# The first product of a macaron block's start: its weights on two transfer queues, and TensorE's order around it

## Chip, cores and metric

One core of a Trainium2 chip runs the whole program in one launch. The metric is the device time of one execution in microseconds, as the median over a number of executions; smaller is better. Beside the timed runs there is one execution with the hardware profiler on.

## What is computed

Tokens x of shape (2, 2048, 256), all in float32, go through three residual steps: half a grouped feed-forward step, a state-space step, and the same feed-forward step again.

```python
x = x + 0.5 * ffn(layernorm(x), W1, b1, W2, b2)
x = x + ssm(layernorm(x), Wi, bi, conv_w, conv_b, Wdt, bdt, A_log, Bm, Cm, Dv, Wo, bo)
x = x + 0.5 * ffn(layernorm(x), W1, b1, W2, b2)
```

The feed-forward step cuts the 4096 tokens into 8 groups of 512. Group g has its own weights, and there is no nonlinearity between its two products:

```python
h1 = einsum('gmh,goh->gmo', xg, W1) + b1[:, None, :]     # 256 -> 1024
h2 = einsum('gmo,gho->gmh', h1, W2) + b2[:, None, :]     # 1024 -> 256
```

The state-space step projects 256 channels to 2 x 512, runs a causal convolution of width 4 and a SiLU over the first half, makes a step size with a softplus, and scans 512 channels with 16 states each over the 2048 tokens of a sequence. The scan's output is gated with SiLU of the other half and projected back to 256 channels; the normalised input times the mean of Dv is added.

## The kernel before

The tokens are worked on in four blocks (s) of 1024, two blocks to a sequence. A block has two halves (h) of 512 tokens, and a half of the tokens is also one group of the feed-forward step: g = 2s + h.

Since the feed-forward step has no nonlinearity, the kernel first multiplies the two weight arrays of a group into one 256 x 256 array. combine(g, k, hh) does this on TensorE: k is one of the two halves of the 1024 inner channels, hh one of the two halves of the 256 input channels, and each call is four matmuls, which in float32 are two passes each. k = 0 and k = 1 add up in the same PSUM tile, pwc. combined(g) brings it to SBUF as wc, scaled by 0.5: ScalarE takes hh = 0, and in group 0 VectorE takes hh = 1. The bias row b1 W2 + b2 is made on TensorE as well. pad_bias copies a group's b1 into a padded tile (GpSimd), bias_pe multiplies it with the second weight array (four matmuls for each k, then one for b2, which lands in the same tile pbc), and bias_act copies the row to SBUF (ScalarE). For group 0 the row is added inside the token product: product(pair, True) multiplies 256 transposed tokens with wc and then spreads the row over the partitions (line 402 and line 298).

A half of the tokens is made ready by settle (statistics on VectorE, two small steps on ScalarE for the root, then the normalisation, one pair of token tiles on VectorE and the other on ScalarE) and by turn (four TensorE transposes for each pair, line 370, and a ScalarE copy to SBUF).

What the core reads at the start is issued in the order of the code. load_x(s, h) issues one transfer of 512 KB of tokens, in pieces of 1 KB. load_w(g, k) issues two transfers of 512 KB, one for each weight array (lines 121 and 122), in pieces of 4 KB. SP's queue gets the first tokens, then the weights of group 0, k = 0 and k = 1, then those of group 1, then wi_sb, the input projection (line 149). ScalarE's queue gets b1 (line 144) and the second half's tokens. GpSimd's queue gets b2 early and, after pad_bias(0), the parameters of the state-space step (load_par).

TensorE's order at the start is the order in which the code is written, by hand. busy(n) issues n matmuls of zeros (line 769). Then come the transposes of the first half, the product for k = 0, the first part of the bias row, the product for k = 1, the second part of the bias row, and then the token product. The transposes of the second half and the weights of group 1 follow, and the first projection of the state-space step.

```python
    busy(12)
    settle(first[0])
    turn(first[0])
    for hh in range(2):
        combine(0, 0, hh)
    settle(first[1])
    pad_bias(0)
    load_par()
    make_sel_rep()
    bias_pe(0, (0,))
    for hh in range(2):
        combine(0, 1, hh)
    combined(0, True)
    bias_pe(0, (1,))
    bias_act(0)
```

Behind the start a loop runs over 256 steps t, one scan of 1024 elements on 128 partitions each (line 691). For each step a plan says which other pieces of work are issued with it; the dictionary PL gives the distance of each piece from a base step, and a name such as nw or tp0 stands there once for all blocks. at(t, fn) puts a piece into the plan, and put_ffn, put_second and put_prepare put whole chains of them. The weights of later groups are issued from the plan, too, by load_w, through SP's queue.

Of the kernel before, what the change touches and what calls it, by code (L numbers as in the profile page):

```python
# [74 lines left out]
def macaron_kernel(ctx: ExitStack, tc: tile.TileContext, x, wi_t, wo_t, wdt_t, par, w1, w2_t, b1, b2, bo, out):  # L75
    nc = tc.nc
    V, S, T, GP = nc.vector, nc.scalar, nc.tensor, nc.gpsimd
# [62 lines left out]
    wo_sb = const.tile([P, NPAIR, DM], F32, name="wo_sb")  # L140

    load_x(0, 0)
    load_w(0, 0)
    S.dma_start(b1_sb, b1.rearrange("p g o -> p (g o)"))
    load_x(0, 1, S)
    load_w(0, 1)
    for k in range(2):
# [619 lines left out]
    def busy(n, warm=warm):  # L767
        for _ in range(n):
            T.matmul(warm[:, :DM], lhsT=zeros[:, :P], rhs=zeros, start=True, stop=True)
# [17 lines left out]
    bias_pe(0, (0,))
    for hh in range(2):
        combine(0, 1, hh)
    combined(0, True)  # L790
    bias_pe(0, (1,))
    bias_act(0)
    make_par_g()
    make_neg_a()
    for pair in range(2):
# [50 lines left out]
    plan = {}

    def at(t, fn, *a, name=None):

        name = name or fn.__name__  # L850
        kind = 3 if name == "fill" else 2 if name in ("dt_pe", "dt_act", "exp_table") else name.endswith("_pe") or name in (
            "product", "project_out", "combine")
        if t % 1:
            kind = 4
        plan.setdefault(int(t), []).append((kind, lambda: fn(*a)))

    def put(t, make, *steps):
# [4 lines left out]
            at(t + d, lambda method=method, a=a: getattr(box[0], method)(*a), name=method)  # L862

    def put_ffn(t, s, h, name):
        put(t, lambda: Ffn(s, h, name), (0, "stats"), (PL["nw"], "newton", GP), (PL["nr"], "normalise", 0, GP),
            (PL["nr"], "normalise", 1, GP), (PL["tp0"], "turn_pe", 0), (PL["ta0"], "turn_act", 0),
            (PL["tp1"], "turn_pe", 1), (PL["ta1"], "turn_act", 1), (PL["bi"], "bias", GP), (PL["pr0"], "product", 0),
            (PL["pr1"], "product", 1), (PL["ad0"], "add_act", 0), (PL["ad0"], "add_gp", 0),
            (PL["ad1"], "add_act", 1), (PL["ad1"], "add_gp", 1))
# [5 lines left out]

    def put_prepare(t, s, q):
        if (s, q) == (0, 1):
            put(t, lambda: Prepare(s, q), (5.5, "inner_pe", 0), (5.5, "inner_pe", 1), (6, "start_xi"), (6, "inner_act", 0),
                (6, "inner_act", 1), (6, "edges"), (6, "centre", 0), (7, "centre", 1),
                (PL["z0"], "tap", 2, 0), (PL["z1"], "tap", 1, 0), (PL["z2"], "tap", 0, 0), (PL["z2"], "gate_u", 0),  # L880
                (PL["z3"], "drive_gp", 0),
                (PL["y0"], "tap", 2, 1), (PL["y1"], "tap", 1, 1), (PL["y2"], "tap", 0, 1), (PL["y2"], "gate_u", 1),
                (PL["y3"], "drive_gp", 1), (PL["y4"], "gate_pe", 0), (PL["y4"], "gate_pe", 1), (PL["y5"], "silu_zs"))
            return
        steps = [(PL["i0"], "inner_pe", 0), (PL["i1"], "inner_pe", 1), (PL["ia"], "start_xi"), (PL["ia"], "inner_act", 0),
                 (PL["ia"], "inner_act", 1), (PL["ed"], "edges"), (PL["ce"], "centre", 0), (PL["ce"], "centre", 1)]
        steps += [(PL["tp"] + n, "tap", k, i)
                  for n, (k, i) in enumerate((k, i) for k in (2, 1, 0) for i in range(NJ2))]
        steps += [(PL["g0"], "gate_pe", 0), (PL["g1"], "gate_pe", 1), (PL["si"], "silu"),
                  (PL["dr"], "drive", GP, 0), (PL["dr"], "drive", GP, 1)]  # L890
# [30 lines left out]
    for s in range(NB):  # L921
# [24 lines left out]
        if s + 1 < NB:
            for h in range(2):
                t = e + PL["f3" + "ab"[h]]
                put_ffn(t, s, h, "f3")
                at(t + PL["st"], store, s, h)  # L950
            g = 2 * s + 2
            for h in range(2):
                at(b + PL[f"lx{h}"] if s > 0 else b + 2 + h, load_x, s + 1, h)
# [4 lines left out]
                at(c + PL["bp"], bias_pe, g + h)
                at(c + PL["cb"], combined, g + h)
                at(c + PL["ba"], bias_act, g + h)  # L960
                at(c + PL["sp"], spread_pe, g + h)
                at(c + PL["sq"], spread_act, g + h)
# [126 lines left out]
```

## Time and profile before

| what | value |
|---|---|
| median of 3 runs | 771.52 us (767.36 to 773.42) |
| profiled execution, its own time | 764.32 us |
| span from its first to its last instruction | 762.5 us |
| mean granted TensorE clock | 0.937 |
| TensorE busy | 642.3 us (84%) |
| VectorE busy | 638.6 us (84%) |
| ScalarE busy | 527.1 us (69%) |
| GpSimd busy | 512.9 us (67%) |
| traffic of the DMA engines | 62.29 MB, mean 82 GB/s |
| first tokens: issue, landing | 0.73 us, 4.7 us |
| weights of group 0 (w1 and w2 of k = 0, then of k = 1): landings | 6.6, 9.8, 11.4 and 12.9 us |
| second half's tokens: issue, landing | 1.22 us, 12.5 us |
| first scan starts | 42.22 us |

Times inside an execution count from the first instruction of the span. A landing is the time of issue and the time from issue to landing that the profile gives. A busy time of TensorE counts passes that overlap in its pipeline, so it isn't work at its peak.

### The profile page before, as it was taken

Reading aid. Unit: us, or ns where it says so; the run is one execution under the profiler, and the core shown is the slowest. Engines: PE = TensorE matmul, PEld = TensorE weight load, DVE = VectorE, ACT = ScalarE, POOL = GpSimd, SP = SyncE. Lnnn points to the kernel's source line nnn. Section 1 sums busy time; section 2 is a strip of 40 time slices with the busy share of each in tenths; the row PEclk is TensorE's granted clock in tenths of the full one; section 3 lists DMA queues with packets and bytes.
Section 4 is the critical chain, followed back from the end, with each engine's and each line's share of the span. In section 5 each row is a group of like instructions: output and inputs, shape, how many; then the busy total and the mean of one; then the engine's idle time right before and its main releaser. Section 6 shows DMA issues by size and latency. Waiting matters only on the chain.

```text
span 762.5 us, 10406 instructions
## 1 busy us (share of the span) xinstructions
PE 642.3 (84%) x3428; PEld 277.1 (36%) x3428; DVE 638.6 (84%) x553; ACT 527.1 (69%) x658; POOL 512.9 (67%) x821
## 2 busy tenths in 40 slices
PE   9999795993879998897888998897697989677966
PEld 7634241440212543542211643353121524212534
DVE  3587777793999989776999989776999999999995
ACT  3467885753899576765899675757699777768631
POOL 5125658899854759979853779989964678753321
PEclk9999799997899999999899999999799999897989
DMA  8274216242122325415122325313122222322101
GB/s 298 72 220 113 55 29 166 56 125 68 28 56 65 74 56 155 135 38 160 40 55 56 73 67 142 112 51 75 37 56 55 56 57 75 92 56 55 29 1 55
DMA packets 42789, 62.29 MB, mean 82 GB/s; under 512 B 12536, under 2 KB 22128, under 8 KB 42736
## 3 DMA queue, kind: packets, MB, share of 16 engines
q1 hardware_dynamic: 41344, 59.84, 28.9%
q0 software_dynamic: 720, 1.24, 0.6%
q8 instruction: 27, 0.44, 0.2%
q10 hardware_dynamic: 672, 0.56, 0.2%
q14 instruction: 26, 0.21, 0.1%
HBM read 24.08 MB, written 4.19 MB: 37 GB/s over the span
## 4 chain that ended last, share of the span: by engine, by line
PE 39%; POOL 22%; DVE 13%; ACT 11%; issue 6%; DMA 6%; SPq 2%; ACTq 0%; DVEq 0%; POOLq 0%
DVE g L691 11%; PE pwc L259 7%; PE py L700 7%; PE po L732 7%; POOL u L530 5%; ACT dec L678 5%; PE pv L662 4%; DMA rep<-dt 3%; PE pf_f L402 3%; PE pxi L488 3%; POOL tap L529 3%; DMA w<-in_w_t 2%; POOL x L414 2%; POOL x L395 2%; PE pz L488 2%
## 5 line engine op out<-in xcount | busy, mean ns | idle before, releaser
L678 ACT ACTIVATE dec<-rep,neg_a 128x1024 f32<-128x1024 f32 (+1 forms) x280 | 287.6, 1059 | 122.4 <-DVE g L691 82.9
L691 DVE TENSOR_TENSOR_SCAN g<-dec,state,pv 128x1024 f32<-128x1024 f32 (+1 forms) x160 | 309.5, 2003 | 26.6 <-PE py L700 13.0
L691 DVE TENSOR_TENSOR_SCAN g<-dec,pv 128x1024 f32<-128x1024 f32 (+1 forms) x128 | 264.9, 2131 | 34.4 <-PE py L700 17.2
L700 PE MATMUL py<-g,wy 128*32 128x512 f32 x1024 | 167.7, 654 | 51.1 <-ACT ev_y L707 35.0
L530 POOL TENSOR_TENSOR u<-u,tap 128x512 f32<-128x512 f32 x90 | 114.2, 1268 | 9.0 <-ACT u L524 1.6
L662 PE MATMUL pv<-v,sel_rep 64*128 64x512 f32 (+1 forms) x256 | 72.8, 663 | 31.9 <-POOL v L630 15.2
L693 POOL COPY state<-g 128x1 f32<-128x1 f32 x160 | 27.5, 185 | 80.0 <-DVE g L691 80.0
L700 PEld LDWEIGHTS py<-g,wy 128*32 128x32 f32 x1024 | 25.2, 111 | 147.4 <-issue 60.6
L711 POOL TENSOR_TENSOR z<-ev_y,z 128x512 f32<-128x512 f32 x31 | 39.6, 1276 | 50.3 <-ACT ev_y L707 50.3
L402 PE MATMUL pf_f<-wc,xnt_f 128*128 128x256 f32 x256 | 66.5, 405 | 5.9 <-ACT ev_f L410 4.3
L529 POOL TENSOR_SCALAR tap<-xi,par_p 128x512 f32<-128x512 f32 x84 | 58.1, 692 | 8.7 <-DMA xi<-xi 5.4
L488 PE MATMUL pz<-xn2t,wi_sb 128*64 128x512 f32 x224 | 61.9, 681 | 0.0
L259 PE MATMUL pwc<-w,w 128*128 128x256 f32 x256 | 60.8, 386 | 0.2 <-ACT dt L94 0.2
L402 PEld LDWEIGHTS pf_f<-wc,xnt_f 128*128 128x128 f32 x256 | 48.0, 197 | 32.5 <-ACT ev_f L410 8.2
L732 PE MATMUL po<-wo_sb,z 64*128 64x256 f32 x448 | 54.6, 391 | 0.8 <-POOL z L711 0.7
L259 PEld LDWEIGHTS pwc<-w,w 128*128 128x128 f32 x256 | 47.1, 190 | 18.4 <-issue 8.9
L488 PE MATMUL pxi<-xn2t,wi_sb 128*64 128x512 f32 x224 | 51.1, 598 | 0.0
L732 PEld LDWEIGHTS po<-wo_sb,z 64*128 64x128 f32 x448 | 43.5, 192 | 16.8 <-issue 10.6
L395 POOL TENSOR_TENSOR x<-x,bc 128x1024 f32<-128x1024 f32 x14 | 33.0, 2355 | 23.4 <-ACT xn_f L361 23.4
L662 PEld LDWEIGHTS pv<-v,sel_rep 64*128 64x128 f32 (+1 forms) x256 | 19.6, 190 | 75.6 <-DVE g L691 35.3
L630 POOL TENSOR_TENSOR v<-u,dt 128x512 f32<-128x512 f32 x28 | 35.0, 1270 | 6.9 <-ACT u L597 6.9
L414 POOL TENSOR_TENSOR x<-ev_f,x 128x512 f32<-128x512 f32 x24 | 30.4, 1269 | 3.1 <-ACT ev_f L410 3.1
(158 smaller groups left out, 745.1 us busy)
## 6 DMA issues: line engine op xcount, KB each, us to landing
rep<-dt SPq DMA_DIRECT2D x496, 64.0 KB, 2.0
w<-in_w SPq DMA_DIRECT2D x16, 512.0 KB, 6.9
w<-in_w_t SPq DMA_DIRECT2D x16, 512.0 KB, 8.7
x<-in_x SPq DMA_DIRECT2D x7, 512.0 KB, 3.9
out<-x SPq DMA_DIRECT2D x6, 512.0 KB, 3.2
wi_sb<-in_wi_t SPq DMA_DIRECT2D x1, 1024.0 KB, 13.8
wo_sb<-in_wo_t SPq DMA_DIRECT2D x2, 512.0 KB, 6.7
out<-x SPq DMA_DIRECT2D x4, 256.0 KB, 2.2
```

What stands on the lines that cost most here:

```text
L259: T.matmul(pt, lhsT=a[:, oc, hh * P : (hh + 1) * P], rhs=b[:, oc, :], start=(k == 0 and oc == 0), stop=(k == 1 and oc == NO // 2 - 1),)
L395: eng.tensor_tensor(self.xs, self.xs, bc[self.g].to_broadcast((P, GT, DM)), ALU.add)
L402: T.matmul(o, lhsT=self.xt[pair][:, hh, k * P : (k + 1) * P], rhs=wc[self.g][:, hh, :], start=(hh == 0), stop=(hh == NH - 1 and not bias))
L414: GP.tensor_tensor(part, self.ev.rearrange("p (a b) -> p a b", a=2), part, ALU.add)
L488: T.matmul(pt[h * HC : (h + 1) * HC, :], lhsT=wi_sb[:, hh, k : k + HC], rhs=xn2t[self.s, h][:, hh, :], start=(hh == 0), stop=(hh == NH - 1))
L529: GP.tensor_scalar(tap, self.xi[:, u, k : k + CH], self.par(C_CW, NK, u, k), 0.0, ALU.mult, ALU.add)
L530: GP.tensor_tensor(self.u[:, u, :], self.u[:, u, :], tap, ALU.add)
L662: T.matmul(t[:, c * CH : (c + 1) * CH], lhsT=sel_rep[r, c if is_wide(s, j) else a, :], rhs=v_sb[s, j // NJ2][r, j % NJ2, :], start=True, s ...
L678: S.activation(decs[t][:, c * w : (c + 1) * w], part, AF.Exp, scale=neg_a[:, i : i + 1])
L691: V.tensor_tensor_scan(g[:, r], dec[:, r], v[:, r], 0.0 if first else state[:, i : i + 1], ALU.mult, ALU.add)
L700: T.matmul(pys[s, j][rows(is_wide(s, j), a, c), :], lhsT=wy[:, column(s, j, a, c, m), :], rhs=gs[a, m][:, c * CH : (c + 1) * CH], start=(m ...
L732: T.matmul(held_po[s, pair][h][:, k * DM : (k + 1) * DM], lhsT=lhsT, rhs=rhs, start=((q, i) == parts[0]), stop=((q, i) == parts[-1]))
```

## The change

Three things are changed.

The transfers at the start: load_w takes a queue for the second weight array. For group 0 this is ScalarE's queue: w1 of k = 0 and k = 1 go on SP's queue behind the first tokens, w2 of k = 0 and k = 1 go on ScalarE's queue, ahead of b1 and of the second half's tokens.

TensorE's order at the start: eleven matmuls of zeros in place of twelve, then the product for k = 0, the transposes of the first half, the whole bias row, and the product for k = 1. ScalarE copies the bias row ahead of wc.

The plan: each chain gets names of its own in PL (f3a.nw, f1b.nw, q2.t3 and so on), each with the value that the shared name had, and the weights of later groups are issued by load_w_part, one array at a time.

```diff
-    def load_w(g, k, pool=None):
+    def load_w(g, k, pool=None, second=nc.sync):
...
         nc.sync.dma_start(a, w1v[:, k * NO // 2 : (k + 1) * NO // 2, :])
-        nc.sync.dma_start(b, w2v[:, k * NO // 2 : (k + 1) * NO // 2, :])
+        second.dma_start(b, w2v[:, k * NO // 2 : (k + 1) * NO // 2, :])
         w_sb[g, k] = (a, b)
...
     load_x(0, 0)
-    load_w(0, 0)
+    for k in range(2):
+        load_w(0, k, second=S)
     S.dma_start(b1_sb, b1.rearrange("p g o -> p (g o)"))
     load_x(0, 1, S)
-    load_w(0, 1)
     for k in range(2):
         load_w(1, k, p5)
     nc.sync.dma_start(wi_sb, wi_t.rearrange("(hh p) d -> p hh d", p=P))
+
+    def load_w_part(g, k, i):
+
+        view = (w1, w2_t)[i][g].rearrange("(p oc) h -> p oc h", p=P)
+        a = wpool.tile([P, NO // 2, DM], F32, tag=f"w{i + 1}", name=f"w{i + 1}_{g}_{k}")
+        nc.sync.dma_start(a, view[:, k * NO // 2 : (k + 1) * NO // 2, :])
+        w_sb[g, k] = (*w_sb.get((g, k), ()), a)
...
-    busy(12)
+    busy(11)
     settle(first[0])
-    turn(first[0])
+    pad_bias(0)
     for hh in range(2):
         combine(0, 0, hh)
+    turn(first[0])
     settle(first[1])
-    pad_bias(0)
     load_par()
     make_sel_rep()
-    bias_pe(0, (0,))
+    bias_pe(0)
+    bias_act(0)
     for hh in range(2):
         combine(0, 1, hh)
     combined(0, True)
-    bias_pe(0, (1,))
-    bias_act(0)
...
-                    for k in range(2):
-                        at(c + PL["lw"], load_w, g + h + 1, k)
+                    for n in range(4):
+                        at(c + PL[f"w{n}"], load_w_part, g + h + 1, n // 2, n % 2)
```

More of the change, by code (lines that the diff above doesn't have):

```diff
@@ L842, in macaron_kernel @@
         load_w(2, k)
-    PL = {'g0': 8, 'g1': 11, 'si': 12, 'po0': 3, 'po1': 7, 'poa': 4, 'c0': 12, 'c1': 28, 'f3a': 13, 'f3b': 17, 'f1a': 20, 'f1b': 30, 'sa': 32, 'sb': 41, 'nw': 0, 'nr': 2, 'tp0': 3, 'ta0': 5, 'tp1': 4, 'ta1': 6, 'bi': 7, 'pr0': 7, 'pr1': 8, 'ad0': 9, 'ad1': 10, 'rs': 3, 'rb': 7, 'i0': 0, 'i1': 0, 'ia': 2, 'ed': 2, 'ce': 3, 'tp': 5, 'dr': 12, 'dv0': 4, 'dv1': 7, 'cb': 8, 'bp': 2, 'ba': 5, 'sp': 8, 'sq': 9, 'lw': 6, 'lx0': 16, 'lx1': 28, 'st': 12, 'r0': 0, 'r1': 4, 'xg0': 2, 'xs0': 5, 'xf0': 7, 'xf1': 16, 'xg1': 8, 'xs1': 14, 'xw': 23, 'xp0': 12, 'xp1': 29, 'xd': 18, 'xr0': 29, 'xb0': 35, 'xr1': 32, 'xb1': 40, 'y0': 11, 'y1': 12, 'y2': 13, 'y3': 17, 'y4': 16, 'y5': 18, 'z0': 6, 'z1': 8, 'z2': 8, 'z3': 10, 'ga': 2, 'gm': 2, 'eo': 3, 'en': 4, 'ep': 6, 'eb': 8, 'u0': 1, 'u1': 1, 'u2': 1, 'u3': 2, 'u4': 3, 'u5': 4, 'u6': 5, 'u7': 5, 'u8': 6, 'u9': 7, 'ua': 11}
+    PL = {'po0': 3, 'po1': 7, 'c0': 12, 'c1': 28, 'f3a': 13, 'f3b': 17, 'f1a': 20, 'f1b': 30, 'sa': 32, 'sb': 41, 'dv0': 4, 'dv1': 7, 'lx0': 16, 'lx1': 28, 'st': 12, 'r0': 0, 'r1': 4, 'xg0': 2, 'xs0': 5, 'xf0': 7, 'xf1': 16, 'xg1': 8, 'xs1': 14, 'xw': 23, 'xp0': 12, 'xp1': 29, 'xd': 18, 'xr0': 29, 'xb0': 35, 'xr1': 32, 'xb1': 40, 'y0': 11, 'y1': 12, 'y2': 13, 'y3': 17, 'y4': 16, 'y5': 18, 'z0': 6, 'z1': 8, 'z2': 8, 'z3': 10, 'ga': 2, 'gm': 2, 'eo': 3, 'en': 4, 'ep': 6, 'eb': 8, 'u0': 1, 'u1': 1, 'u2': 1, 'u3': 2, 'u4': 3, 'u5': 4, 'u6': 5, 'u7': 5, 'u8': 6, 'u9': 7, 'ua': 11, 'f3a.nw': 0, 'f3a.nr': 2, 'f3a.tp0': 3, 'f3a.ta0': 5, 'f3a.tp1': 4, 'f3a.ta1': 6, 'f3a.bi': 7, 'f3a.pr0': 7, 'f3a.pr1': 8, 'f3a.ev0': 9, 'f3a.ad0': 9, 'f3a.ev1': 10, 'f3a.ad1': 10, 'f3a.nr1': 2, 'f3b.nw': 0, 'f3b.nr': 2, 'f3b.tp0': 3, 'f3b.ta0': 5, 'f3b.tp1': 4, 'f3b.ta1': 6, 'f3b.bi': 7, 'f3b.pr0': 7, 'f3b.pr1': 8, 'f3b.ev0': 9, 'f3b.ad0': 9, 'f3b.ev1': 10, 'f3b.ad1': 10, 'f3b.nr1': 2, 'f1a.nw': 0, 'f1a.nr': 2, 'f1a.tp0': 3, 'f1a.ta0': 5, 'f1a.tp1': 4, 'f1a.ta1': 6, 'f1a.bi': 7, 'f1a.pr0': 7, 'f1a.pr1': 8, 'f1a.ev0': 9, 'f1a.ad0': 9, 'f1a.ev1': 10, 'f1a.ad1': 10, 'f1a.nr1': 2, 'f1b.nw': 0, 'f1b.nr': 2, 'f1b.tp0': 3, 'f1b.ta0': 5, 'f1b.tp1': 4, 'f1b.ta1': 6, 'f1b.bi': 7, 'f1b.pr0': 7, 'f1b.pr1': 8, 'f1b.ev0': 9, 'f1b.ad0': 9, 'f1b.ev1': 10, 'f1b.ad1': 10, 'f1b.nr1': 2, 'sa.nw': 0, 'sa.nr': 2, 'sa.tp0': 3, 'sa.ta0': 5, 'sa.tp1': 4, 'sa.ta1': 6, 'sa.rs': 3, 'sa.rb': 7, 'sa.nr1': 2, 'sb.nw': 0, 'sb.nr': 2, 'sb.tp0': 3, 'sb.ta0': 5, 'sb.tp1': 4, 'sb.ta1': 6, 'sb.rs': 3, 'sb.rb': 7, 'sb.nr1': 2, 'q1.i1': 0, 'q1.ia': 2, 'q1.ed': 2, 'q1.ce': 3, 'q1.g0': 8, 'q1.g1': 11, 'q1.si': 12, 'q1.dr': 12, 'q1.t0': 5, 'q1.t1': 6, 'q1.t2': 7, 'q1.t3': 8, 'q1.t4': 9, 'q1.t5': 10, 'q2.i0': 0, 'q2.i1': 0, 'q2.ia': 2, 'q2.ed': 2, 'q2.ce': 3, 'q2.g0': 8, 'q2.g1': 11, 'q2.si': 12, 'q2.dr': 12, 'q2.t0': 5, 'q2.t1': 6, 'q2.t2': 7, 'q2.t3': 8, 'q2.t4': 9, 'q2.t5': 10, 'q3.i0': 0, 'q3.i1': 0, 'q3.ia': 2, 'q3.ed': 2, 'q3.ce': 3, 'q3.g0': 8, 'q3.g1': 11, 'q3.si': 12, 'q3.dr': 12, 'q3.t0': 5, 'q3.t1': 6, 'q3.t2': 7, 'q3.t3': 8, 'q3.t4': 9, 'q3.t5': 10, 'q0.i0': 0, 'q0.i1': 0, 'q0.ia': 2, 'q0.ed': 2, 'q0.ce': 3, 'q0.g0': 8, 'q0.g1': 11, 'q0.si': 12, 'q0.dr': 12, 'q0.t0': 5, 'q0.t1': 6, 'q0.t2': 7, 'q0.t3': 8, 'q0.t4': 9, 'q0.t5': 10, 'q1.i0': 0, 'w0': 6, 'w1': 6, 'w2': 6, 'w3': 6, 'bp0': 2, 'cb0': 8, 'ba0': 5, 'sp0': 8, 'sq0': 9, 'bp1': 2, 'cb1': 8, 'ba1': 5, 'sp1': 8, 'sq1': 9, 'pe0': 4, 'pe1': 4, 'pa0': 4, 'pa1': 4}
@@ L852, in at @@
             "product", "project_out", "combine")
-        if t % 1:
-            kind = 4
+        order = round(t % 1 * 10)
+        kind = 4 if order == 5 else kind + order / 10
         plan.setdefault(int(t), []).append((kind, lambda: fn(*a)))
@@ L864, in put_ffn @@
     def put_ffn(t, s, h, name):
[L865 to L869, printed above, removed]
-    def put_second(t, s, h):
-        put(t, lambda: Second(s, h), (0, "stats"), (PL["nw"], "newton", GP), (PL["nr"], "normalise", 0, GP),
-            (PL["nr"], "normalise", 1, GP), (PL["tp0"], "turn_pe", 0), (PL["ta0"], "turn_act", 0),
-            (PL["tp1"], "turn_pe", 1), (PL["ta1"], "turn_act", 1), (PL["rs"], "residual"), (PL["rb"], "residual_bias"))
+        c = name + "ab"[h] + "."
+        put(t, lambda: Ffn(s, h, name), (0, "stats"), (PL[c + "nw"], "newton", GP), (PL[c + "nr"], "normalise", 0, GP),
+            (PL[c + "nr1"], "normalise", 1, GP), (PL[c + "tp0"], "turn_pe", 0), (PL[c + "ta0"], "turn_act", 0),
+            (PL[c + "tp1"], "turn_pe", 1), (PL[c + "ta1"], "turn_act", 1), (PL[c + "bi"], "bias", GP),
+            (PL[c + "pr0"], "product", 0), (PL[c + "pr1"], "product", 1), (PL[c + "ev0"], "add_act", 0),
+            (PL[c + "ad0"], "add_gp", 0), (PL[c + "ev1"], "add_act", 1), (PL[c + "ad1"], "add_gp", 1))
+    def put_second(t, s, h):
+        c = "s" + "ab"[h] + "."
+        put(t, lambda: Second(s, h), (0, "stats"), (PL[c + "nw"], "newton", GP), (PL[c + "nr"], "normalise", 0, GP),
+            (PL[c + "nr1"], "normalise", 1, GP), (PL[c + "tp0"], "turn_pe", 0), (PL[c + "ta0"], "turn_act", 0),
+            (PL[c + "tp1"], "turn_pe", 1), (PL[c + "ta1"], "turn_act", 1), (PL[c + "rs"], "residual"),
+            (PL[c + "rb"], "residual_bias"))
     def put_prepare(t, s, q):
@@ L884, in put_prepare @@
             return
[L885 to L890, printed above, removed]
+        c = f"q{q}."
+        steps = [(PL[c + "i0"], "inner_pe", 0), (PL[c + "i1"], "inner_pe", 1), (PL[c + "ia"], "start_xi"),
+                 (PL[c + "ia"], "inner_act", 0), (PL[c + "ia"], "inner_act", 1), (PL[c + "ed"], "edges"),
+                 (PL[c + "ce"], "centre", 0), (PL[c + "ce"], "centre", 1)]
+        steps += [(PL[f"{c}t{n}"], "tap", k, i) for n, (k, i) in enumerate((k, i) for k in (2, 1, 0) for i in range(NJ2))]
+        steps += [(PL[c + "g0"], "gate_pe", 0), (PL[c + "g1"], "gate_pe", 1), (PL[c + "si"], "silu"),
+                  (PL[c + "dr"], "drive", GP, 0), (PL[c + "dr"], "drive", GP, 1)]
         if q == 0:
@@ L943, in macaron_kernel @@
             for h in range(2):
-                at(t + PL["poa"], add_out_act, s, pair, h)
-                at(t + PL["poa"], add_out_gp, s, pair, h)
+                at(t + PL[f"pe{pair}"], add_out_act, s, pair, h)
+                at(t + PL[f"pa{pair}"], add_out_gp, s, pair, h)
         if s + 1 < NB:
@@ L957, in macaron_kernel @@
                     at(c + n, combine, g + h, k, hh)
[L958 to L962, printed above, removed]
+                at(c + PL[f"bp{h}"], bias_pe, g + h)
+                at(c + PL[f"cb{h}"], combined, g + h)
+                at(c + PL[f"ba{h}"], bias_act, g + h)
+                at(c + PL[f"sp{h}"], spread_pe, g + h)
+                at(c + PL[f"sq{h}"], spread_act, g + h)
                 if g + h + 1 < G:
-                    for k in range(2):
-                        at(c + PL["lw"], load_w, g + h + 1, k)
+                    for n in range(4):
+                        at(c + PL[f"w{n}"], load_w_part, g + h + 1, n // 2, n % 2)
                 put_ffn(b + PL["f1" + "ab"[h]], s + 1, h, "f1")
```

## The prediction

> **What bounds the kernel now.** I read the page first, then the chain of waits, then the start of the execution engine by engine, since the code that differs in what it issues is the code ahead of the first scan.
>
> ```profile
> span 762.5 us, 10406 instructions
> PE 642.3 (84%) x3428; PEld 277.1 (36%) x3428; DVE 638.6 (84%) x553; ACT 527.1 (69%) x658; POOL 512.9 (67%) x821
> ```
>
> The page says that no one engine is the bound over the whole span: TensorE and VectorE are both busy 84% of it. What a change at the start is worth must be read at the start. The chain of waits there (start, length, what):
>
> ```profile
> 1.09 8.38 PE warm L769 x24
> 9.47 0.87 PE ptr_f L370 x8
> 10.34 3.46 PE pwc L259 x16
> ...
> 19.10 1.06 PE pf_f L402 x4
> ```
>
> From 1.09 to 30.55 us the chain holds nothing but TensorE, and the first scan stands behind it at 42.22 us. So the start is as long as TensorE's list, provided that what the list reads is there. The timeline of TensorE (start, length, then the group; its length holds the pipeline's tail, so I use the distances between starts):
>
> ```profile
> 8.66 0.81 PE L769 MATMUL warm<-b_pad 128*128 128x256 f32 x3
> 9.30 1.04 PE L370 MATMUL ptr_f<-ident,xn_f 128*128 128x128 f32 x8
> 10.18 3.62 PE L259 MATMUL pwc<-w,w 128*128 128x256 f32 x16
> 13.73 0.64 PE L280 MATMUL pbc<-w,b_pad 128*32 128x256 f32 x8
> 14.29 3.72 PE L259 MATMUL pwc<-w,w 128*128 128x256 f32 x16
> 17.95 0.64 PE L280 MATMUL pbc<-w,b_pad 128*32 128x256 f32 x8
> 18.52 0.59 PE L285 MATMUL pbc<-b_sb,ident 8*1 8x256 f32 x2
> 19.03 1.13 PE L402 MATMUL pf_f<-wc,xnt_f 128*128 128x256 f32 x4
> ```
>
> The reader is to see two things. TensorE has no hole. And the bias row's second part (17.95 to 19.03) stands between the end of the weights' product and the first use of that product. In this time ScalarE and VectorE bring the product out of PSUM:
>
> ```profile
> 15.57 1.09 ACT L361 ACTIVATE xn_f<-x,nm_f,rs_f 128x256 f32<-128x256 f32 x2 [0.82 <-DVE nm_f L344]
> 18.05 0.38 ACT L270 ACTIVATE wc<-pwc 128x256 f32<-128x256 f32 x1 [1.39 <-PE pwc L259]
> 18.47 0.42 DVE L268 TENSOR_SCALAR wc<-pwc 128x256 f32<-128x256 f32 x1 [2.09 <-ACT wc L270]
> ```
>
> Last, the transfers: each microsecond's traffic (the last column is GB/s; the rows between read 318, 305 and 255), and packets and MB of SP's queue (q1) and ScalarE's (q10) from 5 to 11 us.
>
> ```profile
> 2.00:3.00 1.00, 1.00 (x4) 0.73 (x4) 0.00 (x0) 0.01 (x1) 0.87 (x5) 1.00 0.57 159
> 3.00:4.00 1.00, 1.00 (x4) 0.82 (x3) 0.00 (x0) 0.00 (x0) 0.92 (x3) 1.00 1.07 364
> 4.00:5.00 1.00, 1.00 (x4) 0.82 (x3) 0.23 (x1) 0.00 (x0) 0.84 (x7) 1.00 1.02 404
> ...
> 8.00:9.00 1.00, 1.00 (x6) 0.89 (x5) 0.64 (x2) 0.99 (x2) 0.00 (x0) 1.00 0.94 368
> 9.00:10.00 1.00, 1.00 (x10) 0.90 (x9) 0.00 (x0) 0.06 (x1) 0.46 (x2) 1.00 1.04 413
> ```
>
> ```profile
> q1 hardware_dynamic: 433, 1.57, 72.6%
> q10 hardware_dynamic: 492, 0.49, 23.9%
> ```
>
> From 3 us on the 16 DMA engines are near full. The two queues share them about packet for packet (433 to 492) and not byte for byte (1.57 to 0.49 MB): tokens travel in packets of 1 KB, weights in packets of 4 KB. The first weights' second array (issued 1.76, 8.0 us to landing) lands at 9.8, just ahead of its use at 10.18. The start is thus bound by TensorE, with the transfers close behind.
>
> **The change, part by part.** *The plan's table* gets more names with the same values, and load_w_part issues the two arrays of each half in the order of before. Every engine's list after the start is the same. Cost 0, nothing hides it because nothing differs.
>
> *One warm-up matmul less.* Three passes lie between 8.66 and 9.30, 0.216 us each, and a warm-up is two passes: TensorE is free at 9.30 - 0.43 = 8.87 us.
>
> *Order on TensorE.* Before, from 9.30: transposes 0.88, first product 3.55, bias 0.56, second product 3.66, bias 0.57, b2's row 0.51, together 9.73 to the use at 19.03. The same pieces stand in the new order, so 9.73 again. But the second product is now last, and its way out of PSUM has no cover: ScalarE starts 0.10 after TensorE could go on (17.95 to 18.05), takes 0.38, and some 0.07 go to the signal: 0.55 us of hole. VectorE's half ends at 18.89, 0.94 behind the 17.95; the first use's two passes take as long as the rest of that wait, so nothing is added. The bias row ready earlier buys nothing: its copy ended at 19.51 and its reader stood at 20.09. So the use comes at t0 + 9.73 + 0.55 = t0 + 10.28, t0 being the start of the first product, and the shift is t0 - 8.75. With t0 at its floor of 8.87 the change already costs 0.12 us: taking the product ahead of the transposes can't gain more than the one warm-up, and the hole takes that back.
>
> *Transfers, which set t0.* Adding up the traffic rows (1 to 2 us: 12): 0.17 MB at 3.0 us, 0.54 at 4, 0.94 at 5, 1.26 at 6, 1.56 at 7, 1.82 at 8, 2.19 at 9, 2.60 at 10, 3.01 at 11. Now the first product needs w1 on SP's queue behind the first tokens (0.52 + 0.52 = 1.05 MB) and w2 at the head of ScalarE's. Until SP's queue is that far, ScalarE's moves at least as many bytes (1.05 MB, byte for byte: 2.10 in all) and at most packet for packet: 640 packets, which are both w2 arrays, b1 and 256 packets of the second tokens, 1.34 MB: 2.39 in all. To this comes what runs ahead behind the array and its receipt: w1 landed before at 6.6, when 1.44 MB had moved, of which 1.08 (tokens, w1, b1) and about 0.17 of the second tokens were due: 0.19; w2 at 9.8, at 2.52 MB with 1.61 and about 0.43 due: 0.48. So 2.29 to 2.87 MB, by the sums above 9.25 to 10.66 us. The packet row says that the share lies near packet for packet: 2.39 + 0.19 = 2.58 MB is the nearest, 9.95; I take t0 = 10.0, its larger overrun being set off by what a second queue may put into the row of 159 GB/s. TensorE then idles from 8.87 to 10.0.
>
> The Trainium skill speaks against this part: "DMA: Bandwidth & Descriptors", Rules for kernel authors, says that spreading transfers over SP, ACT and GpSimd does not help bandwidth, since all run on the same 16 engines and interleave. The rows agree from 3 us on (shares 0.94 to 1.07) and leave room only at 2 to 3 us (0.57); by the rule alone t0 would be the upper 10.66.
>
> *What stands behind it.* The first tokens now share with 4 KB packets. Packet for packet, their 512 packets go with 1.05 + 0.03 + 0.13 MB, 1.73 in all, 7.7 us, and 8.5 with the overrun of their landing before (0.26 MB), against 4.7. Their normalised form came 4.2 us after the landing (4.77 to 9.00), so at 11.9 to 12.7; the transposes want it at 10.0 + 3.5 = 13.5: covered, by 0.8 us at the least. b1 (behind both w2) is due at 7.4 to 8.4 by the same count; POOL needs it at 9.1, and after it come only load_par's issues, whose last reader on VectorE (par_g) ended 0.66 us ahead of the next thing VectorE had to wait for. The second tokens: 896 packets a queue, 3.70 MB, with overrun 3.9 to 4.2, 13.1 to 13.8 us against 12.5. On ScalarE their normalisation, then the bias row's copy (0.37), now stand ahead of wc: 13.8 + 4.16 + 0.37 = 18.3, and wc is due at 10.0 + 9.83 = 19.8: covered by 1.5 us. SP's later issues wait for earlier landings as before, its queue never runs dry, and wi_sb (26.3) is read at 31.8.
>
> **Sum:** 10.0 + 10.28 - 19.03 = +1.25 us, from +0.12 (t0 8.87) to +1.9 (t0 10.66). The scan's start hangs on this list, and no later wait of the chain is one that absorbs it. On the profiled execution (764.32 us, span 762.5) that is 765.6. That execution lies 7.2 us below the median of the runs shown, 771.52, which is what is to be predicted: 772.8.
>
> **Rivals.** *The weights are there when TensorE is free.* For it: the row of 159 GB/s leaves 0.2 MB of room, and less run-ahead is possible. Against: even byte for byte 2.29 MB take until 9.25. Price: +0.1, 771.6 us.
>
> *The hole slows TensorE's clock.* It idles about 1.1 us, up to 1.8. For it: passes took 0.427 us until 7.05 and 0.216 after, so a fall costs double; one or two of the profile's clock steps (3.41 us) at half speed give +1.7 to +3.4 on top: 774.5 to 776.2. Against: in the stretch 471.3 to 474.7 TensorE was busy 1.81 of 3.40 us and the granted clock stayed 1.00; it fell after 75.3 to 78.7 with 0.42 busy. It decides where a hole leaves less than some 40% of a step. "TensorE: Matmul & The Clock Gate" in the Trainium skill, Part 1, puts the fall behind a whole idle window of about 3.4 us; by that the price would be 0.
>
> *The second tokens starve: slower.* If ScalarE's queue gets its turn only when SP's is empty, x of the second half lands with the last of SP's bytes, at about 23 us. ScalarE then reaches wc at 23 + 4.16 + 0.37 and the first use waits until 28.0: +9.0, 780.5 us. It decides from a landing after 15.3. Against: the 492 packets to 433; before, those tokens had the same rival queue and landed at 12.5.
>
> *Nothing happens at all*, the start's shift being lost in a later wait: 771.5, not to be told from the forecast in the total.
>
> **How the numbers follow.** Forecast 0.60 (+0.6 to +1.9), weights in time or no effect 0.23, clock 0.08, starved 0.05, and 0.04 for a set of runs that comes out low by more than 1%. One per cent is 7.7 us, about what a measurement of this kernel can tell from no change; only the starved case and the last one pass it: faster 0.04, same 0.91, slower 0.05. The range takes the runs' own spread, since it is wider than the shift: lowest 767.36, and 764.32 in the profiled execution, give 766; 773.42 + 1.9, and part of the clock's price, give 777.
>
> **What would show it.** Right: TensorE idle for 0.4 to 1.8 us ahead of the first pwc, ended by a DMA; a hole of about 0.55 us ahead of the first pf_f, ended by ScalarE's wc; pf_f between 19.1 and 21.0; first tokens at 7.5 to 8.5, second ones at 13 to 14; all later groups equal in count and length. Wrong: pf_f before 19.0, a landing of the second tokens past 15.3, or a granted clock below 1 between 8 and 30 us.

## The result: 0.7% slower, and the profile after

The changed kernel takes 773.29 us (median of 20 runs, 768.74 to 778.88). The kernel before, run 20 times beside it, takes 768.66 us (763.38 to 773.42). The ratio is 1.0067 with a 95% interval of 1.0045 to 1.0089, so the change costs 3.5 to 6.8 us, some 5 in the middle. The profiled execution of the changed kernel took 773.02 us.

The page says as little of the cause as the one before did: the engines do the same work in a longer span.

```profile
span 771.2 us, 10400 instructions
PE 640.8 (83%) x3426; PEld 275.9 (36%) x3426; DVE 638.6 (83%) x553; ACT 527.2 (68%) x658; POOL 514.6 (67%) x821
```

The chain of waits at the start (start, length, what) has changed its first owner:

```profile
2.25 16.71 DMA x<-in_x
18.96 0.02 issue
18.99 1.41 DVE st_f L329 x4
...
22.09 1.09 ACT xn_f L368 x2
23.18 0.26 ACT brow L299
23.44 0.29 ACT wc L277
23.73 0.04 issue
23.78 1.68 PE pf_f L409 x4
```

Before, TensorE alone stood here from 1.09 us on. Now the chain begins with the transfer of the second half's tokens, which ScalarE issues at 2.25 and which lands at 18.96. Behind it come that half's statistics and normalisation, then ScalarE's copies of the bias row and of wc, and only then TensorE's first use of the product. The timeline of TensorE shows the same from its side:

```profile
10.16 3.69 PE L266 MATMUL pwc<-w,w 128*128 128x256 f32 x16 [1.08 <-DMA w<-in_w]
13.69 1.04 PE L377 MATMUL ptr_f<-ident,xn_f 128*128 128x128 f32 x8
14.65 1.07 PE L287 MATMUL pbc<-w,b_pad 128*32 128x256 f32 x16
15.65 0.59 PE L292 MATMUL pbc<-b_sb,ident 8*1 8x256 f32 x2
16.17 3.72 PE L266 MATMUL pwc<-w,w 128*128 128x256 f32 x16
23.78 1.68 PE L409 MATMUL pf_f<-wc,xnt_f 128*128 128x256 f32 x4 [3.88 <-ACT wc L277]
```

The first product starts at 10.16, and everything that TensorE multiplies ahead of the use is done at 19.9. The use itself starts at 23.78, where 19.03 stood before: 4.75 us later. In the bracket stands the wait, 3.88 us, and its releaser, the copy of wc. A second loss follows. The first group of line 409 takes 1.68 us instead of 1.13, because TensorE's clock was at half from 24.2 us on, just behind the wait (the column ahead of the last two is the granted clock, the last one GB/s):

```profile
20.60:24.00 3.40, 0.22 (x1) 0.23 (x2) 1.73 (x9) 2.13 (x6) 1.46 (x6) 1.00 0.70 162
24.20:27.60 3.40, 3.40 (x15) 1.73 (x14) 1.74 (x16) 0.26 (x1) 1.15 (x5) 0.50 0.02 5
```

One step of 3.41 us at half clock makes the stretch from the first use to the second half's transposes (31.88) 8.10 us long; before it was 6.52 (19.03 to 25.55). So 4.75 + 1.58 = 6.33, and the first scan starts at 48.54 instead of 42.22, 6.32 us later.

The transfers explain the landing. These are the queues' packets, MB and time from 2 to 6 us, then from 10 to 16 us (q1 is SP's, q10 ScalarE's):

```profile
q10 hardware_dynamic: 146, 0.53, 48.9%
q1 hardware_dynamic: 462, 0.51, 43.4%
...
q1 hardware_dynamic: 509, 1.87, 79.6%
q10 hardware_dynamic: 512, 0.49, 23.6%
```

In the first stretch ScalarE's queue moved 146 packets, hardly more than one of its two weight arrays (128 pieces of 4 KB each), while SP's moved 462, nearly all of them pieces of the first tokens. This stretch is not all of one kind. Its parts from 3.0 to 4.5 us and from 5 to 6 us:

```profile
q10 hardware_dynamic: 71, 0.29, 74.4%
q1 hardware_dynamic: 77, 0.08, 17.2%
...
q1 hardware_dynamic: 219, 0.26, 73.0%
q10 hardware_dynamic: 21, 0.05, 14.4%
```

From 3.0 to 4.5 us the queues took turns packet for packet. SP's queue got ahead before that (125 packets to 28 from 2 to 3 us) and again from 5 to 6 us, when ScalarE's queue had its first array nearly through and the second hardly begun. From 10 to 16 us the queues took turns packet for packet again, 509 to 512. By then ScalarE's queue held the second tokens, in pieces of 1 KB, and each of them had to let a 4 KB packet of SP's weights pass: 0.49 MB in six microseconds, beside 1.87 MB of SP's, nearly all of it weights of the next group, which are read only from 32.8 us on.

### The profile page after: what moved, and what is told of

Read it like the earlier page. It is cut to its first block, busy times and chain, and to the rows that moved or that the text cites. A ratio compares the mean times of both kernels' runs of the same rounds, so it can differ in the third digit from the quotient of the medians.

```text
span 771.2 us, 10400 instructions
## 1 busy us (share of the span) xinstructions
PE 640.8 (83%) x3426; PEld 275.9 (36%) x3426; DVE 638.6 (83%) x553; ACT 527.2 (68%) x658; POOL 514.6 (67%) x821
## 4 chain that ended last, share of the span: by engine, by line
PE 40%; POOL 22%; DVE 12%; ACT 10%; DMA 8%; issue 6%; SPq 1%; ACTq 0%; DVEq 0%; POOLq 0%
DVE g L698 9%; PE py L707 8%; PE po L739 7%; PE pwc L266 6%; POOL u L537 5%; ACT dec L685 5%; PE pv L669 4%; DMA w<-in_w_t 4%; PE pf_f L409 3%; PE pxi L495 3%; POOL tap L536 3%; POOL x L421 2%; PE pz L495 2%; DMA x<-in_x 2%; POOL x L402 2%
## 5 line engine op out<-in xcount | busy, mean ns | idle before, releaser
L707 PE MATMUL py<-g,wy 128*32 128x512 f32 x1024 | 164.4, 655 | 52.3 <-ACT ev_y L714 34.6
L669 PEld LDWEIGHTS pv<-v,sel_rep 64*128 64x128 f32 (+1 forms) x256 | 19.5, 189 | 75.2 <-DVE g L698 32.4
L329 DVE BATCH_NORM_STATS2 st_f<-x 128x6 f32<-128x256 f32 x64 | 22.4, 410 | 16.6 <-DMA x<-in_x 16.4
```

The costliest lines, as they stand in the source:

```text
L669: T.matmul(t[:, c * CH : (c + 1) * CH], lhsT=sel_rep[r, c if is_wide(s, j) else a, :], rhs=v_sb[s, j // NJ2][r, j % NJ2, :], start=True, s ...
L707: T.matmul(pys[s, j][rows(is_wide(s, j), a, c), :], lhsT=wy[:, column(s, j, a, c, m), :], rhs=gs[a, m][:, c * CH : (c + 1) * CH], start=(m ...
```

## The experiments

Two theories stood at first. **The late tokens**: the second half's tokens land late, ScalarE's copy of wc is queued behind their normalisation, and the clock falls in the wait. **The order**: TensorE's new order, with the product last and its way out of PSUM uncovered, costs most of it. Four kernels separate them. In the short diffs, lines marked with a minus are those of the changed kernel unless said otherwise.

**order_only**: TensorE's new order and the new plan, the transfers as before.

```diff
     load_x(0, 0)
-    for k in range(2):
-        load_w(0, k, second=S)
+    load_w(0, 0)
     S.dma_start(b1_sb, b1.rearrange("p g o -> p (g o)"))
     load_x(0, 1, S)
+    load_w(0, 1)
```

> TensorE's new order and the plan's new names as in the changed kernel, the transfers issued as before. Theory of the late tokens: the loss came from the second half's tokens (landed 18.96 instead of 12.5 us) with ScalarE's copy of wc queued behind them, and from the clock that fell in TensorE's wait. Here the first weights land at 9.8 and the tokens at 12.5 again, so the first product starts at 9.9 and its use at 9.9 + 10.28 = 20.2 us (19.03 before, 23.78 in the changed kernel); no clock step below 1 ahead of 40 us; first scan near 43.4 (42.2 and 48.5); ratio to before about 1.0015, not beyond 1.003. Rival theory, the order costs: TensorE's order alone gives most of the loss, use of the product past 22 us, ratio about 1.006.

Measured: ratio 1.0019 (0.9997 to 1.0040). On TensorE:

```profile
10.10 3.69 PE L266 MATMUL pwc<-w,w 128*128 128x256 f32 x16 [1.10 <-DMA w<-in_w_t]
20.30 1.16 PE L409 MATMUL pf_f<-wc,xnt_f 128*128 128x256 f32 x4 [0.47 <-ACT wc L277]
```

The use comes at 20.30, 1.27 us behind the kernel before, the first scan at 43.51, 1.30 behind; the clock does not fall ahead of 85 us. The hole is there as forecast (0.47 us, ended by ScalarE's copy), and it is small. As the main cause the order is out: alone it costs about a fifth of the 6.3 us.

**queues_only**: the transfers of the changed kernel, the order of before.

```diff
-    busy(11)
+    busy(12)
     settle(first[0])
-    pad_bias(0)
+    turn(first[0])
     for hh in range(2):
         combine(0, 0, hh)
...
-    bias_pe(0)
-    bias_act(0)
+    bias_pe(0, (0,))
     for hh in range(2):
         combine(0, 1, hh)
     combined(0, True)
+    bias_pe(0, (1,))
+    bias_act(0)
```

> The transfers issued as in the changed kernel, TensorE's, ScalarE's and VectorE's order as before. Theory of the late tokens: they land near 19 us again, their normalisation on ScalarE ends at 23.2, and ScalarE copies wc only then: use of the product at 23.6 to 24.0 us, as in the changed kernel (23.78). TensorE's work ahead of it (transposes from 11.7 us, since the first tokens land at 7.4) ends at about 21.4, a hole of some 2.3 us instead of 3.9; first scan at 46.8 to 48.5; ratio 1.005 to 1.007. Rival theory, the order costs: use of the product at 19 to 21 us and ratio under 1.002.

Measured: ratio 1.0054 (1.0030 to 1.0079), first scan at 48.06, 5.85 us behind.

```profile
18.70 1.41 DVE L329 BATCH_NORM_STATS2 st_f<-x 128x6 f32<-128x256 f32 x4 [7.59 <-DMA x<-in_x]
...
22.89 0.36 ACT L277 ACTIVATE wc<-pwc 128x256 f32<-128x256 f32 x1
...
23.30 1.84 PE L409 MATMUL pf_f<-wc,xnt_f 128*128 128x256 f32 x4 [2.38 <-ACT wc L277]
```

The use comes at 23.30, a little ahead of what was expected, by the same wait with the same releaser. So the queues alone give nearly the whole loss, and TensorE's order hardly matters once they are in place: the two costs don't add, since the hole and the late start lie inside the wait for the tokens.

**settle_late**: the changed kernel, with the second half's statistics and normalisation behind the copy of wc.

```diff
     turn(first[0])
-    settle(first[1])
     load_par()
...
     combined(0, True)
+    settle(first[1])
```

> The changed kernel with one step moved: the statistics and the normalisation of the second half's tokens stand behind the copy of wc on ScalarE and VectorE instead of ahead of it. Theory of the late tokens: what costs is that wc is queued behind them, not that they land late. They land near 19 us as before, wc is copied when the second product ends (19.9), its use starts at about 20.4 instead of 23.78, the clock does not fall, and the first scan comes at 43.5 to 44.5; ratio 1.001 to 1.003. Rival theory, the order costs (or the queues cost through something else than the tokens): use near 23.8 us, ratio near 1.0067.

Measured: ratio 1.0029 (1.0005 to 1.0053), first scan at 43.73, 1.51 us behind.

```profile
19.72 0.38 ACT L277 ACTIVATE wc<-pwc 128x256 f32<-128x256 f32 x1 [3.28 <-PE pwc L266]
20.13 0.42 DVE L275 TENSOR_SCALAR wc<-pwc 128x256 f32<-128x256 f32 x1 [8.94 <-ACT wc L277]
20.15 1.16 PE L409 MATMUL pf_f<-wc,xnt_f 128*128 128x256 f32 x4 [0.47 <-ACT wc L277]
20.48 1.40 DVE L329 BATCH_NORM_STATS2 st_f<-x 128x6 f32<-128x256 f32 x4
```

The tokens are still late, but nothing that TensorE waits for is queued behind them: wc is copied as soon as the product ends, and the use comes at 20.15. Moving one line took back 4.8 of the 6.3 us. What cost was thus not the late landing alone, but the place of the copy of wc behind it in ScalarE's list. Nor did that place cost much alone: order_only has it too, with tokens in time.

**tokens_ahead**: the changed kernel, with b1 and the second tokens ahead of the weights on ScalarE's queue.

```diff
     load_x(0, 0)
-    for k in range(2):
-        load_w(0, k, second=S)
     S.dma_start(b1_sb, b1.rearrange("p g o -> p (g o)"))
     load_x(0, 1, S)
+    for k in range(2):
+        load_w(0, k, second=S)
```

> The changed kernel with b1 and the second half's tokens ahead of both w2 arrays on ScalarE's queue instead of behind them. Theory of the late tokens: both halves' tokens land by 8 us, the first weights at about 10 to 10.5, so the first product starts at 10 to 10.6 and its use at 20.3 to 20.9 us; no fall of the clock; first scan at 43.5 to 44.1; ratio 1.001 to 1.003. Rival theory, the order costs: use at 23 us or later, ratio near 1.006.

Measured: ratio 1.0103 (1.0067 to 1.0138), first scan at 50.18, 7.96 us behind. The expectation missed, and the slowest kernel of all is the lesson on the queues:

```profile
14.92 5.53 PE L266 MATMUL pwc<-w,w 128*128 128x256 f32 x16 [6.91 <-DMA w<-in_w_t]
...
26.97 1.16 PE L409 MATMUL pf_f<-wc,xnt_f 128*128 128x256 f32 x4 [0.47 <-ACT wc L277]
```

```profile
q1 hardware_dynamic: 328, 1.19, 74.0%
q10 hardware_dynamic: 399, 0.41, 28.9%
```

The second fence is the traffic from 6 to 10 us. The second tokens now hold the head of ScalarE's queue with 1 KB packets, and the first w2 stands behind them until 14.8 us. I had the tokens land at 8; they landed at 11.6. From 3.5 to 4.5 us ScalarE's queue, with b1 through and the tokens issued at 1.21, sent 9 packets beside 274 of SP's; then its tokens met SP's weights. TensorE idled 6.91 us, its clock fell for two steps, and the first product itself took 5.53 us. A queue's second item can be no earlier than its first allows, whichever of the two is the needed one.

**keep_warm**: the changed kernel, with matmuls of zeros in the wait.

```diff
+    busy(8)
     for pair in range(2):
         first[0].product(pair, True)
```

> The changed kernel with eight matmuls of zeros (busy(8), some 3.5 us at full clock) put into TensorE's wait ahead of the first use of the product. Theory: of the 6.33 us by which the first scan comes later, 4.75 are the wait for the second half's tokens and 1.6 the clock, which fell to half for one step of 3.41 us because TensorE stood idle from 19.9 to 23.8. Expected: use of the product at 23.8 again, no clock step below 1 ahead of 60 us, the stretch from that use to the second half's transposes 6.5 us instead of 8.1, first scan at 46.9; ratio 1.004 to 1.006. Rival, the slow passes came from something else (a shared PSUM or SBUF port): 8.1 us and a first scan at 48.5 again.

Measured: ratio 1.0057 (1.0037 to 1.0078), first scan at 46.74, 4.52 us behind.

```profile
23.52 1.16 PE L409 MATMUL pf_f<-wc,xnt_f 128*128 128x256 f32 x4 [0.51 <-ACT wc L277]
...
30.07 1.09 PE L377 MATMUL ptr_f<-ident,xn_f 128*128 128x128 f32 x8
```

The stretch from the first use to the transposes is 6.55 us again instead of 8.10, and no clock step falls ahead of 88 us. Of the 1.80 us by which the first scan comes earlier than in the changed kernel, 1.55 are the clock; the rest goes with a landing 0.3 us earlier in this execution. The rival (a shared port) is out.

**w1_on_act**: the two weight arrays exchanged between the queues, one profile. It asks why ScalarE's queue moved so little in the first 4 us.

```diff
-        nc.sync.dma_start(a, w1v[:, k * NO // 2 : (k + 1) * NO // 2, :])
-        second.dma_start(b, w2v[:, k * NO // 2 : (k + 1) * NO // 2, :])
+        second.dma_start(a, w1v[:, k * NO // 2 : (k + 1) * NO // 2, :])
+        nc.sync.dma_start(b, w2v[:, k * NO // 2 : (k + 1) * NO // 2, :])
```

> The changed kernel with the two weight arrays exchanged between the queues: w1 of both halves on ScalarE's queue, w2 on SP's behind the first tokens. Open from the trace of the changed kernel: in its first 3.5 us of traffic a weight packet took 212 to 257 ns instead of 160, so ScalarE's queue came to b1 and the tokens only at 9 us. If the place in the queues makes them slow (two queues starting at once), w1's packets are as slow from 2 to 5 us, first tokens land near 7.4 and second ones near 19, and the start is the same within 0.5 us. If it is the array w2, w1's packets take 160 ns, and b1 and the second tokens land 1 to 2 us earlier, with the first scan 1 to 2 us earlier.

Measured: first scan at 48.68, and from 2 to 6 us:

```profile
q10 hardware_dynamic: 145, 0.53, 49.5%
q1 hardware_dynamic: 468, 0.51, 42.1%
```

145 packets against 146: it isn't the array. The 0.53 MB are some 130 pieces of 4 KB, and they took 0.495 x 16 engines x 4 us: some 240 ns a piece here.

**b2_on_act**: b2's small transfer on ScalarE's queue instead of GpSimd's, one profile.

```diff
-    GP.dma_start(b2_sb, b2)
...
     S.dma_start(b1_sb, b1.rearrange("p g o -> p (g o)"))
+    S.dma_start(b2_sb, b2)
```

> The changed kernel with b2's small transfer (8 KB) issued by ScalarE behind b1 instead of by GpSimd at 1.28 us. Open so far: weight packets take 200 to 300 ns instead of 160 somewhere between 2 and 8 us in every trace, with one queue and with two, and with either weight array. Theory: GpSimd's own transfer, whose descriptors software writes, slows them while it is under way (it lands at 6.6 to 8.7). Then packets take 160 ns from 2 us on, the traffic of 3 to 5 us rises from 240 to 400 GB/s, first tokens land at 6 instead of 7.4, second ones near 17.5 instead of 19, and the first scan comes 1 to 1.5 us earlier than in the changed kernel (48.54). Rival, something else slows them (the memory's first pages, or the tokens' small pieces): same rows within 10%, first scan within 0.3 us.

Measured: first scan at 49.66; the traffic from 3 to 5 us is as low as in the changed kernel (261 and 232 GB/s there):

```profile
3.00:4.00 1.00, 1.00 (x4) 0.81 (x3) 0.00 (x0) 0.00 (x0) 0.82 (x7) 1.00 0.99 288
4.00:5.00 1.00, 1.00 (x4) 0.81 (x3) 0.00 (x0) 0.00 (x0) 0.00 (x0) 1.00 0.77 225
```

So it isn't GpSimd's transfer either. What makes early weight packets slow stays open. The first scan came 1.1 us later than in the changed kernel, which neither theory had: the second tokens, now ScalarE's fifth transfer, were issued only at 7.26 us instead of 2.25 and landed at 19.4, and the clock was at half for two steps (22.2 to 29.0).

Two kernels try for a version that beats both. **weights_first** puts all of the start on SP's queue, with the second tokens behind the weights, and lets the bias row cover the product's way out of PSUM:

```diff
     load_x(0, 0)
-    for k in range(2):
-        load_w(0, k, second=S)
     S.dma_start(b1_sb, b1.rearrange("p g o -> p (g o)"))
-    load_x(0, 1, S)
+    for k in range(2):
+        load_w(0, k)
+    load_x(0, 1)
...
     turn(first[0])
-    settle(first[1])
     load_par()
     make_sel_rep()
-    bias_pe(0)
-    bias_act(0)
     for hh in range(2):
         combine(0, 1, hh)
     combined(0, True)
+    bias_pe(0)
+    bias_act(0)
+    settle(first[1])
```

> Order of the first product ahead of the transposes kept; one queue: SP's carries the first tokens, the weights of group 0, then the second half's tokens; ScalarE's carries b1 alone; the bias row is multiplied behind the second product, so that it covers the product's way out of PSUM; the second half's normalisation stands behind the copies of wc and the bias row. Theory (packet for packet sharing makes a queue slow that stands beside another): with one queue the first weights land at 8 to 9 us instead of 9.8, the first product starts at 8.9 to 9.2, its use at 18.6 to 18.9 (19.03 before), the second tokens land at 12.5 to 13.5 and hold up nothing; first scan at 41.8 to 42.1; ratio 0.999 to 1.000, not to be told from no change in the total. Rival, two queues share nothing that matters here: first weights at 9.8 as before, use at 19.6 or later.

Measured: the start is better than forecast, the first scan at 41.41, 0.80 us ahead of the kernel before. The whole is not: ratio 1.0020 (1.0000 to 1.0040).

```profile
8.76 3.69 PE L266 MATMUL pwc<-w,w 128*128 128x256 f32 x16 [1.07 <-DMA w<-in_w_t]
...
18.23 1.13 PE L409 MATMUL pf_f<-wc,xnt_f 128*128 128x256 f32 x4
```

The first product starts at 8.76 and its use 9.47 us later, without a hole. With the same kernel and b2 on ScalarE's queue (**weights_first_b2**, the edit of b2_on_act), the start was the same:

> weights_first with b2's transfer on ScalarE's queue behind b1 instead of on GpSimd's. If GpSimd's transfer is what slows the early packets, the first weights land at 7.5 to 8 instead of 8.7, the first product starts as soon as the warm-up ends and the clock is up, the use of the product comes at 17.5 to 18 (18.23 without this), first scan at 40.7 to 41.2 (41.42 without), ratio 0.998 to 1.001. If not: the same start as weights_first within 0.3 us, and the ratio within its interval of 1.000 to 1.004.

Measured: first scan at 41.32, ratio 0.9995 (0.9966 to 1.0024), no change that can be told.

**weights_ahead** goes further and puts the first half's weights ahead of the first tokens, with both products ahead of the transposes:

```diff
-    load_x(0, 0)
-    for k in range(2):
-        load_w(0, k, second=S)
     S.dma_start(b1_sb, b1.rearrange("p g o -> p (g o)"))
-    load_x(0, 1, S)
+    load_w(0, 0)
+    load_x(0, 0)
+    load_w(0, 1)
+    load_x(0, 1)
...
-    busy(11)
+    busy(6)
     settle(first[0])
     pad_bias(0)
-    for hh in range(2):
-        combine(0, 0, hh)
+    for k in range(2):
+        for hh in range(2):
+            combine(0, k, hh)
+    combined(0, True)
     turn(first[0])
...
     bias_pe(0)
     bias_act(0)
+    settle(first[1])
```

> As weights_first, with the weights of the first half ahead of the first tokens on SP's queue (w1, w2 of k = 0, first tokens, w1, w2 of k = 1, second tokens), six matmuls of zeros, and TensorE's order: both products, transposes, bias row, use. Theory (the start is as long as TensorE's 9.7 us list behind the landing of the first weights): they land at 6.2 to 7.5, the products start there, the second half's weights land at 10 to 11, first tokens at 8 to 8.5 and their normalised form at 12.3 to 12.8, ahead of the transposes; use of the product at 16.5 to 17.5 (19.03 before), first scan at 39.7 to 40.7, ratio 0.997 to 0.998. Rival, the start is bound by the traffic as a whole: use at 18.5 to 19.5, ratio 1.000.

Measured: ratio 1.0016 (0.9994 to 1.0037), first scan at 43.14, 0.93 us behind. The rival came nearer: the start is bound by what the transfers bring, though the use, at 19.96, lies behind the rival's 18.5 to 19.5, too.

```profile
8.20 3.69 PE L266 MATMUL pwc<-w,w 128*128 128x256 f32 x16 [1.70 <-DMA w<-in_w_t]
13.95 3.69 PE L266 MATMUL pwc<-w,w 128*128 128x256 f32 x16 [2.06 <-DMA w<-in_w_t]
...
19.96 1.13 PE L409 MATMUL pf_f<-wc,xnt_f 128*128 128x256 f32 x4
```

The product starts 2 us earlier than in the changed kernel, but each of its halves then waits for its weights. GpSimd's parameter transfers also start earlier, since they stand behind the shorter warm-up, and run beside the second half's weights.

Over the six experiments other than weights_first and weights_first_b2 whose times were compared, the first scan's shift and the loss go together (1.30, 1.51, 0.93, 4.52, 5.85 and 7.96 us at the first scan; 1.5, 2.2, 1.2, 4.4, 4.1 and 7.9 us by the ratios). Where the 0.8 us that weights_first gains at the start are lost later is not settled: its interval just allows no change, and single profiled executions differ by several microseconds behind the start.

## Why the prediction was right, and where it was not

The time was forecast at 772.8 and came out at 773.3, within 1%, and the sign of the small shift was right. The agreement to half a microsecond is luck: the three runs it started from had a median of 771.52, 2.9 us above the 768.66 of twenty, and the shift was put at +1.25 where 3.5 to 6.8 were measured. Two errors of opposite sign met. Two of the prediction's own signs of being wrong came true: the second tokens landed past 15.3, and the clock fell between 8 and 30 us.

*The plan's table and load_w_part: nothing.* order_only holds these edits, too, and its first scan is 1.30 us late, which the order explains.

*Start of the first product, t0 = 10.0.* Measured 10.16, ended by a DMA as said; with the transfers of before 10.10. Part of the agreement is luck, too: the sum had both queues move about as many packets until then, but from 2 to 10 us SP's moved 807 and ScalarE's 399.

*The list of 9.73 us and the hole of 0.55.* order_only: 10.10 to 20.30, 10.20 against 10.28, with a hole of 0.47 ended by ScalarE. The sum of the forecast, +1.25, is what order_only shows: +1.27 at the use, +1.30 at the first scan. So the forecast was right for TensorE's order.

*First tokens at 7.7 to 8.5 us.* Measured 7.4, and they held up nothing.

*Second tokens at 13.1 to 13.8, b1 at 7.4 to 8.4, "covered by 1.5 us".* This is the step that failed. b1 landed at 11.8 and the second tokens at 18.96, and the cover of 1.5 us became a wait of 3.88. The term mis-sized was the turns that ScalarE's queue would get: packet for packet from the first microsecond. That ratio came from 5 to 11 us, when ScalarE's queue held 1 KB packets and SP's 4 KB packets. It held in the changed kernel from 10 to 16 us (509 to 512), and with the sizes exchanged from 3.0 to 4.5 us (71 to 77). But from 2 to 6 us as a whole it was 146 to 462: the count knew neither the head start of SP's queue nor the microsecond between ScalarE's two arrays. I also took the traffic sums of before (364 and 404 GB/s from 3 to 5 us) for a start that moved 261 and 232. Both put the second tokens behind: their queue still had some 100 weight packets and b1 to send when the first tokens were through.

*The rival "the second tokens starve".* Its place, its condition and the way to its price were right, its chance of 0.05 and its landing at 23 were not. It decides from a landing after 15.3, the landing was 18.96, and 18.96 + 4.16 + 0.37, then the copy of wc, gives a use at about 23.9 (measured 23.78). It needed no starved queue, as the prediction had it: a queue that comes late to its tokens and then takes turns was enough.

*The rival "the hole slows the clock".* It was priced at 1.7 to 3.4 us for the short hole ahead of the first product, and there the clock stayed up. It fell in the other hole, ahead of the use, which the late tokens made 3.9 us long, and cost 1.58. The estimate that the clock falls where less than some 40% of a step is busy fits both holes: TensorE was busy 2.33 of 3.41 us from 7.15 to 10.56, and the clock stayed; it was busy 0.43 from 20.80 to 24.21, and the clock fell. I treated the two rivals as alternatives; the one brought the other.

## What to carry to other kernels

A load moved to a second queue does not only leave the first queue: it stands ahead of what the second queue carried, and what is pushed back there is fed at the pace of turns against all that the first queue still holds. Ask of each item pushed back which instruction reads it, and what that engine has in its list behind that instruction; here a copy of 0.38 us behind a late normalisation cost more than the whole new order. A forecast of landings from a count of packets needs the sharing of the queues in the same situation (sizes, number of queues, first microseconds), not from a later stretch.

## What the runs showed of the hardware

Two queues took turns packet for packet whatever the sizes, 71 to 77 with 4 KB packets on ScalarE's queue and 1 KB packets on SP's, 509 to 512 with the sizes exchanged. But a queue whose next transfer had long been issued did not always move packets. In the six traces with group 0's w2 or w1 on ScalarE's queue ahead of the tokens, that queue moved 16 to 22 packets from 5 to 6 us, between two weight arrays, beside 210 to 238 of SP's. In tokens_ahead it moved 9 beside 274 from 3.5 to 4.5 us, between b1 and the tokens. Why is open.

Early weight packets were slow as well. From 2 to 6 us the 0.53 MB of ScalarE's queue, some 130 pieces of 4 KB, took 0.489 x 16 x 4 us, some 240 ns a piece; from 10 to 16 us the 1.87 MB of SP's, some 457 pieces, took 0.796 x 16 x 6 us, some 170 ns. This cause is open, too; neither the array nor GpSimd's transfer is it.

The clock fell in a shorter idle time than I had thought. In queues_only, TensorE waited 2.38 us, and it was busy 1.02 of the 3.41 us from 20.16 to 23.57, when the clock fell; the first use ran into the step at half clock:

```profile
20.16:23.57 3.41, 1.02 (x10) 0.35 (x4) 2.01 (x11) 2.12 (x6) 1.98 (x8) 1.00 0.79 205
23.57:26.98 3.41, 3.41 (x14) 1.65 (x14) 1.89 (x17) 0.26 (x1) 1.01 (x5) 0.50 0.02 5
```

The Trainium skill ("TensorE: Matmul & The Clock Gate", Part 1) has the clock fall after at least one idle window of about 3.4 us. Here a wait of 2.38 us in a partly busy stretch was enough, so the measurement decides: a whole idle window is not needed. Which share of idle time is needed stays open. If the twelve traces are cut into stretches of 3.41 us that end where the clock changes, every full-clock stretch with TensorE busy less than 40% was followed by a fall, and none with more than 66%. In between there are both: a fall after 1.85 us busy (queues_only, from 125.97), none after 1.39 us (weights_first_b2, from 173.84).

The skill's rule that a second issuing queue brings no bandwidth ("DMA: Bandwidth & Descriptors", Rules for kernel authors) agrees with the traces: from 2 to 10 us SP's and ScalarE's queues together moved 2.68 MB in the changed kernel, 2.58 in the kernel before and 2.60 in weights_first. The first product's weights landed at 10.0, 9.8 and 8.7 us.
